# First cross attention in 64-row parts: scores, key norms and the last keys

## The chip, the cores and the metric

The kernel runs on one core of a Trainium2 chip. The metric is the device time of one execution in microseconds. Five engines work side by side and meet at semaphores: TensorE (PE; its weight loads are shown as PEld), VectorE (DVE), ScalarE (ACT), GpSimd (POOL) and SyncE (SP), which issues DMAs.

TensorE multiplies a stationary operand (lhsT, rows times columns) by a moving one (rhs, rows times N). [...] `128*64` in a profile line means 128 rows and 64 columns; "128x289" behind it is the moving operand, so N is 289. Everything is float32, and each float32 matmul of the program appears as two instructions.

## The reference

Six layers act on x (64 batches of 32 rows, width 256): cross attention, self attention, a mixture of 64 experts, a second cross attention, a latent self attention, a feed-forward layer. The change is within the first layer:

```python
xn = layernorm(x, ln_x_g, ln_x_b)          # context, 257 rows
ln = layernorm(latents, ln_l_g, ln_l_b)    # 32 rows
q = ln @ Wq                                # 16 heads of 64
kv = concat([xn @ Wkv, ln @ Wkv], axis=1)  # 289 keys
sim = einsum('bhid,bhjd->bhij', rmsnorm(q, qn_g) * 64 ** -0.5, rmsnorm(k, kn_g))
sim = where(padded_mask, sim, -max)
out = softmax(sim) @ v ;  return out @ Wout + bout
```

## The kernel before

**Stages.** `before` (the method, about the first 1,600 us) runs the first cross attention, the self attention and the routing; `experts` and `after` follow. In `before` there are 64 steps s, one for each batch; four batches make a tile t of 128 rows, with b = s mod 4. PE's instructions run in the order in which the program is written (a manual schedule). The other engines' order, and which engine an `nc.any` copy falls to (DVE or ACT), is set by a scheduler at build time.

**One step s** does, on PE: `keys(s+2)`, one slot, the transposes of `weigh(s)`, `norms(s+2)`, `values(s)`, `spread(s+2)`, a slot, `scores(s+2)`, `turn(s+3)`, and a third slot unless b is 3. A slot moves each pending generator one `yield` on: those of the queries of the next tile and of the output projection, self attention and routing of tiles that are done.

- `keys` (L160 psA<-xT,wk): 8 pairs of heads; for each, 2 accumulating matmuls give the pair's 128 key dimensions by 289 keys. ACT and DVE copy to kT in turn; after each fourth pair, ACT squares four pairs (L1164) into sq[0] and sq[1]. L1147 and L1148 fetch, by two DMAs on SP, the last 33 keys' rows (32 latents, one context row) into one of three buffers c3.
- `norms` (L1176): sums of squares over a head's 64 dimensions, by a 128 x 32 selector. 8 matmuls of form `128*32`: 4 column groups, 2 accumulating matmuls in each. Then a maximum on DVE (L1184) and a logarithm on ACT (L1185) give nk.
- `spread` (L1197, `32*128`): copies each norm to 32 rows; ACT takes exp(-0.5 .) into rk (L1198).
- `scores` (L1210): for each pair of heads one matmul of form `128*64`. Its stationary operand is qbd, in which the two heads' queries are block-diagonal, with zeros elsewhere. Two pairs fill the two column halves, so 8 matmuls fill 4 PSUM banks. DVE multiplies each bank by rk (L1217), POOL adds the mask (L1218), and `softmax_rows` follows.
- `weigh` (`keyed`, L195): 12 transposes give the weights with keys on partitions: 128, 128 and 33 keys (L196 copies them out; the last go to atl, whose other rows are zero).
- `values` (`weighed`): for each half kc of the 256 dimensions, 3 accumulating matmuls `128*128` with N = 512: two L160 psY<-at,cx and one L160 psY<-atl,c over the zero-padded c3. L205 copies the result to yT after each kc.
- `heads_out` reads yT by head (L160 psY<-yT,wv).
- `queries`, sixth slot: L1090 transposes q, and L1097 copies the parts of 64 rows into qbd.

PSUM has 8 banks, and `bank()` hands them out in a ring. qbd, c3 and atl are set to zero once by POOL (L373).

## Time and profile before

| What | Time or share |
|---|---|
| Median of 3 runs | 2926.83 us (2924.55 to 2929.37) |
| Profiled execution, its own time | 2931.93 us |
| Span of its instructions | 2930.2 us |
| PE busy | 2748.5 us, 94% |
| DVE, ACT, POOL busy | 56%, 42%, 29% |
| PE busy from 100 to 1580 us | 1434.47 of 1480 us, granted clock 1.00 |
| DVE, ACT, POOL busy, same stretch | 841.16, 743.97, 548.48 us |

A row of the timeline gives the start, how long the group lasts to the end of its last instruction, the engine, line, operation, result <- operands, shape and count. [...]

### The profile page before, as it was taken

How to read it: one execution, taken by the hardware profiler on the slowest of the kernel's cores; microseconds unless marked ns; L12 is line 12 of the kernel's file. 1: busy time of each engine (PE TensorE's matmuls, PEld its weight loads, DVE VectorE, ACT ScalarE, POOL GpSimd, SP SyncE). 2: the span in 40 equal slices, each digit the busy share in tenths (PEclk: the TensorE clock that was granted, in tenths of full speed). 3: DMA queues.
4: the chain of work that ended last, by engine and by line, in shares of the span. 5: the costliest groups of instructions: out<-in, count | busy, mean ns of one | idle time of the engine just before them, and what ended most of it. 6: DMA issues, size and time to landing. Idle time of an engine off the chain costs nothing. (4 is left out here: it accounts for less than half of the span.)

```text
span 2930.2 us, 56527 instructions
## 1 busy us (share of the span) xinstructions
PE 2748.5 (94%) x22362; PEld 1882.0 (64%) x22362; DVE 1649.3 (56%) x4401; ACT 1235.5 (42%) x3366; POOL 840.6 (29%) x819
## 2 busy tenths in 40 slices
PE   5999999999999999999999589999999999999995
PEld 3556666656666666666666368777677777777773
DVE  4445566556655655555555423356666666666664
ACT  3444554554455545445544223243333333333331
POOL 5322344234333423442342100222222122212010
PEclk8999999999999999999999789999999999999997
DMA  7000000000000000000000368521112212222110
GB/s 259 15 13 17 29 31 29 17 29 27 28 18 26 25 20 18 18 16 17 16 12 14 113 212 274 167 64 55 54 53 57 56 48 59 56 54 48 39 34 5
DMA packets 130956, 156.86 MB, mean 54 GB/s; under 512 B 20952, under 2 KB 113859, under 8 KB 130692
## 3 DMA queue, kind: packets, MB, share of 16 engines
q1 hardware_dynamic: 109188, 119.64, 13.1%
q0 software_dynamic: 12288, 25.21, 3.4%
q10 hardware_dynamic: 9216, 8.39, 0.8%
q8 instruction: 177, 2.90, 0.4%
q14 instruction: 87, 0.71, 0.1%
HBM read 121.63 MB, written 37.75 MB: 54 GB/s over the span
## 5 line engine op out<-in xcount | busy, mean ns | idle before, releaser
L160 PE MATMUL psA<-xT,wk 128*128 128x289 f32 x2048 | 516.6, 410 | 26.6 <-ACT xT L1136 16.5
L160 PEld LDWEIGHTS psA<-xT,wk 128*128 128x128 f32 x2048 | 386.7, 191 | 146.6 <-issue 37.0
L741 POOL DMA_INDIRECT y<-oute,idx x128 | 130.7, 1021 | 677.0 <-DVE x L752 475.3
L1218 POOL TENSOR_TENSOR rk<-rk,mb 128x1156 f32<-128x1156 f32 x64 | 158.0, 2469 | 433.7 <-DVE rk L1217 420.4
L160 PE MATMUL psY<-at,cx 128*128 128x512 f32 x512 | 248.1, 607 | 0.0
L160 PE MATMUL psA<-at,cx 128*128 128x512 f32 x512 | 236.2, 604 | 0.2 <-ACT at L1325 0.2
L160 PE MATMUL psY<-xT,qk 128*128 128x257 f32 x1024 | 234.4, 381 | 0.0
L160 PEld LDWEIGHTS psY<-xT,qk 128*128 128x128 f32 x1024 | 189.4, 190 | 28.6 <-issue 3.5
L205 ACT COPY yT<-psY 128x512 f32<-128x512 f32 x127 | 74.3, 585 | 241.0 <-PE psY L160 241.0
L1307 ACT ACTIVATE sim<-psY,mx 128x257 f32<-128x257 f32 x256 | 120.7, 473 | 129.5 <-DVE mx L1306 129.3
L176 ACT ACTIVATE rk<-rk,mx 128x289 f32<-128x289 f32 x256 | 134.0, 525 | 95.9 <-DVE mx L174 95.9
L160 PEld LDWEIGHTS psY<-at,cx 128*128 128x128 f32 x512 | 92.5, 190 | 121.5 <-issue 94.8
L1164 ACT ACTIVATE sq<-kT 128x1156 f32<-128x1156 f32 x128 | 148.9, 1164 | 18.6 <-DVE kT L1161 16.4
L160 PEld LDWEIGHTS psA<-at,cx 128*128 128x128 f32 x512 | 91.9, 189 | 97.4 <-issue 82.8
L606 POOL DMA_INDIRECT buf<-z,fi x128 | 126.4, 988 | 95.0 <-DVE fi L603 56.5
L1306 DVE TENSOR_REDUCE mx<-psY 128x1 f32<-128x257 f32 x256 | 102.5, 413 | 79.2 <-PE psY L160 79.2
L1337 DVE SCALAR_TENSOR_TENSOR yT<-at,xT,psA 128x512 f32<-128x512 f32 x128 | 94.3, 746 | 81.5 <-PE psA L160 80.0
L1210 PE MATMUL psB<-kT,qbd 128*64 128x289 f32 x1024 | 140.0, 415 | 0.0
L1159 ACT COPY kT<-psA 128x289 f32<-128x289 f32 x256 | 98.5, 388 | 95.8 <-PE psA L160 95.5
L160 PE MATMUL psY<-atl,c 128*128 128x512 f32 x256 | 130.7, 592 | 0.0
L160 PE MATMUL psY<-yT,wv 128*64 128x128 f32 x2048 | 120.5, 275 | 0.0
L1217 DVE TENSOR_TENSOR rk<-psB,rk 128x289 f32<-128x289 f32 x256 | 111.4, 451 | 15.2 <-ACT rk L1198 8.0
(256 smaller groups left out, 5181.3 us busy)
## 6 DMA issues: line engine op xcount, KB each, us to landing
cx<-in_ctx SPq DMA_DIRECT2D x128, 256.0 KB, 2.7
we<-in_m_ew SPq DMA_DIRECT2D x64, 384.0 KB, 5.0
xT<-in_ctxT SPq DMA_DIRECT2D x64, 257.0 KB, 3.1
buf<-zero SPq DMA_DIRECT2D x32, 256.0 KB, 3.9
be<-buf SPq DMA_DIRECT2D x64, 128.0 KB, 4.1
oute<-oe ACTq DMA_DIRECT2D x64, 128.0 KB, 4.8
mu<-in_mask SPq DMA_DIRECT2D x16, 128.5 KB, 3.0
x<-in_x SPq DMA_DIRECT2D x16, 128.0 KB, 3.7
```

The source lines that it names most:

```text
L160: self.nc.tensor.matmul(ps, lhsT=lhs[i], rhs=rhs[i], start=(i == 0), stop=(i == n - 1))
L176: nc.scalar.activation(sim[:, g, :], sim[:, g, :], AF.Exp, bias=mx[:, g : g + 1], accum_out=sm[:, g : g + 1])
L606: d = nc.gpsimd.indirect_dma_start(out=self.buf[:, :], out_offset=bass.IndirectOffsetOnAxis(ap=fi[:, k : k + 1], axis=0), in_=z[:, 0, :], ...
L741: nc.gpsimd.indirect_dma_start(out=y, out_offset=None, in_=self.oute[:, :], in_offset=bass.IndirectOffsetOnAxis(ap=self.idx[:, t, k : k + ...
L1159: nc.scalar.copy(kT[:, p, :], ps[:, :JK])
L1164: nc.scalar.activation(sq[p // 4], kT[:, p - 3 : p + 1, :], AF.Square)
L1210: nc.tensor.matmul(ps[odd * DH : (odd + 1) * DH, :JK], lhsT=qbd[:, 2 * g + odd, b, :, :].rearrange("p a b -> p (a b)"), rhs=kT[:, 2 * g + ...
L1217: nc.vector.tensor_tensor(sim[:, g, :], ps[:, :JK], sim[:, g, :], ALU.mult)
L1218: nc.gpsimd.tensor_tensor(sim, sim, mb[:, b, :].unsqueeze(1).to_broadcast([P, 4, JK]), ALU.add)
L1306: nc.vector.tensor_reduce(mx[:, g : g + 1], ps[:, :J], AX.X, ALU.max, negate=True)
L1307: nc.scalar.activation(sim[:, g, :], ps[:, :J], AF.Exp, bias=mx[:, g : g + 1], accum_out=sm[:, g : g + 1])
L1337: nc.vector.scalar_tensor_tensor(self.yT[:, c, :, b * S : (b + 1) * S], self.at[:, 2, :].rearrange("p (h i) -> p h i", h=H), xT[:, c, J - ...
```

## The change

Heads 2p and 2p+1 (even and odd) now lie apart, on row halves 0 to 63 and 64 to 127.

- `qbd` is replaced by qT, the transposed queries without the zeros, in a tile with two buffers; two copies of 128 partitions take the place of four of 64.
- `scores`: 16 matmuls of form `64*32` in place of 8 of `128*64`. In each half of the heads, 4 pairs p go to 4 column groups and even and odd go to the two row halves and to two banks.
- `norms`: even heads' sums go to PSUM rows 0 to 63, odd heads' to rows 64 to 127, as the new order of heads needs. 16 matmuls of form `64*32`, 4 accumulating in each of 4 parts (row half 0 with column groups 0 and 1, row half 64 with 2 and 3); two banks, two DVE maxima on 64 partitions each.
- The last 33 keys lie twice, on rows 0 to 32 and 64 to 96: `softmax_rows` writes their weights a second time with one more DVE operation, and the third group of transposes takes 128 columns in place of 33. c3 holds dimensions 0 to 127 on the first row half, 128 to 255 on the second (4 DMAs in place of 2).
- `weighed`: 2 matmuls `128*128` for each kc, then for kc = 0 and kc = 1 one matmul each of form `64*128` on the two row halves, then both copies to yT.
- rk becomes one of three fixed tiles of 4 x 384, set to zero once; at has 3 parts, atl is gone; `heads_out` follows the new order of heads in yT.

```diff
     def norms(self, s):
...
+        ps = [k.bank("psB") for _ in range(2)]
+        for p in range(4):
+            for half in range(2):
+                for odd in range(2):
+                    r, q = slice(DH * odd, DH * odd + DH), DH * odd + 32 * half
+                    nc.tensor.matmul(
+                        ps[odd][q : q + 32, :JK],
+                        lhsT=k.pair[p][r, :],
+                        rhs=sq[half][r, p, :],
+                        start=(p == 0),
+                        stop=(p == 3),
+                    )
+        nk = kp.tile([P, JK], F32, name="nk")
         for odd in range(2):
...
+            r = slice(DH * odd, DH * odd + DH)
+            nc.vector.tensor_scalar(nk[r, :], ps[odd][r, :JK], float(DH) * 1e-16, None, ALU.max)
         nc.scalar.activation(nk, nk, AF.Ln)
...
     def scores(self, s):
...
+        sim = whole[:, :, :JK]
+        for half in range(2):
+            ps = [k.bank("psB") for _ in range(2)]
+            for p in range(4):
+                for odd in range(2):
+                    r = slice(DH * odd, DH * odd + DH)
+                    nc.tensor.matmul(
+                        ps[odd][p * S : (p + 1) * S, :JK],
+                        lhsT=qT[r, 4 * half + p, b * S : (b + 1) * S],
+                        rhs=kT[r, 4 * half + p, :],
+                        start=True,
+                        stop=True,
+                    )
             for odd in range(2):
...
+                g = 2 * half + odd
+                nc.vector.tensor_tensor(sim[:, g, :], ps[odd][:, :JK], sim[:, g, :], ALU.mult)
         nc.gpsimd.tensor_tensor(sim, sim, mb[:, b, :].unsqueeze(1).to_broadcast([P, 4, JK]), ALU.add)
-        k.softmax_rows(sim, JK)
+        k.softmax_rows(sim, JK, whole[:, :, 2 * P + 64 : 2 * P + 64 + S + 1])
...
     def softmax_rows(self, sim, n, twice=None):
...
         nc.vector.reciprocal(sm, sm)
+        if twice is not None:
+            m = twice.shape[2]
+            nc.vector.tensor_tensor(
+                twice, sim[:, :, n - m :], sm.unsqueeze(2).to_broadcast([P, 4, m]), ALU.mult
+            )
...
     def weighed(self, yT, b, at, values, tail=None):
...
+        ps = [self.bank("psY") for _ in range(2)]
+        n = len(at)
         for kc in range(2):
...
+            for i in range(n):
+                nc.tensor.matmul(
+                    ps[kc],
+                    lhsT=values[i][:, kc * P : (kc + 1) * P],
+                    rhs=at[i],
+                    start=(i == 0),
+                    stop=(i == n - 1 and tail is None),
+                )
+        if tail is not None:
+            for kc in range(2):
+                r = slice(64 * kc, 64 * kc + 64)
+                nc.tensor.matmul(ps[kc], lhsT=tail[1][r, :], rhs=tail[0][r, :], start=False, stop=True)
+        for kc in range(2):
+            nc.any.tensor_copy(
+                yT[:, kc, :, b * S : (b + 1) * S], ps[kc].rearrange("p (h i) -> p h i", h=H)
+            )
...
     def keys(self, s):
...
-        nc.sync.dma_start(c3[:S, :], self.own[t][0][b * S : (b + 1) * S, 0, :])
-        nc.sync.dma_start(c3[S : S + 1, :], self.xl[s : s + 1, 0, :])
+        for c in range(2):
+            r, d = 64 * c, slice(c * P, (c + 1) * P)
+            nc.sync.dma_start(c3[r : r + S, :], self.own[t][0][b * S : (b + 1) * S, 0, d])
+            nc.sync.dma_start(c3[r + S : r + S + 1, :], self.xl[s : s + 1, 0, d])
```

More of the change, by code (lines that the diff above doesn't have):

```diff
@@ L43 @@
 C_PAIR = C_TRI + P
-C_SPREAD = C_PAIR + 2 * 32
+C_SPREAD = C_PAIR + 4 * 32
 C_B8 = C_SPREAD + P
@@ L61, in constants @@
     c[:, C_TRI:C_PAIR] = r[:, None] < r[None, :]
-    for a in range(2):
-        at = C_PAIR + a * 32
-        c[:, at : at + 32] = (2 * a + r[:, None] // DH) == np.arange(32)[None, :]
+    for a in range(4):
+        c[:, C_PAIR + a * 32 + a] = 1.0
     c[:, C_SPREAD:C_B8] = (r[:, None] % 32) == (r[None, :] // S)
@@ L166, in add_to_x, with softmax_rows @@
         nc.vector.tensor_tensor(xt, xt, ps, ALU.add)
-    def softmax_rows(self, sim, n):
+    def softmax_rows(self, sim, n, twice=None):
         nc = self.nc
@@ L179, in softmax_rows, with keyed @@
         nc.vector.reciprocal(sm, sm)
+        if twice is not None:
[3 more added lines that the diff above has]
+            )
         for g in range(4):
             nc.vector.tensor_scalar(sim[:, g, :], sim[:, g, :], sm[:, g : g + 1], None, ALU.mult)
-    def keyed(self, sim, sizes, tail=None):
+    def keyed(self, sim, sizes):
         nc = self.nc
-        at = self.atp.tile([P, len(sizes) - (tail is not None), 512], F32, name="at")
-        at = [at[:, j, :] for j in range(at.shape[1])]
-        if tail is not None:
-            at.append(tail)
+        at = self.atp.tile([P, len(sizes), 512], F32, name="at")
         k0 = 0
@@ L195, in keyed, with weighed, heads_out @@
                 nc.tensor.transpose(ps[:n, g * P : (g + 1) * P], sim[:, g, k0 : k0 + n], self.ident)
-            nc.any.tensor_copy(at[j][:n, :], ps[:n, :])
+            nc.any.tensor_copy(at[:n, j, :], ps[:n, :])
             k0 += n
-        return at if tail is not None else [at[j][:n, :] for j, n in enumerate(sizes)]
-    def weighed(self, yT, b, at, values):
-        for kc in range(2):
-            ps = self.bank("psY")
-            self.product(ps, [v[:, kc * P : (kc + 1) * P] for v in values], at)
-            self.nc.any.tensor_copy(
-                yT[:, kc, :, b * S : (b + 1) * S], ps.rearrange("p (h i) -> p h i", h=H)
+        return [at[:n, j, :] for j, n in enumerate(sizes)]
+    def weighed(self, yT, b, at, values, tail=None):
+        nc = self.nc
+        ps = [self.bank("psY") for _ in range(2)]
+        n = len(at)
+        for kc in range(2):
+            for i in range(n):
[13 more added lines that the diff above has]
+                yT[:, kc, :, b * S : (b + 1) * S], ps[kc].rearrange("p (h i) -> p h i", h=H)
             )
-    def heads_out(self, t, yT, wv, wo, bias):
+    def heads_out(self, t, yT, wv, wo, bias, split=False):
         nc = self.nc
@@ L217, in heads_out @@
                     h = 2 * (4 * half + p) + odd
+                    at = 8 * half + 4 * odd + p if split else h
                     self.product(
@@ L220, in heads_out @@
                         [wv[:, k, h * DH : (h + 1) * DH] for k in range(2)],
-                        [yT[:, k, h, :] for k in range(2)],
+                        [yT[:, k, at, :] for k in range(2)],
                     )
@@ L302, in run @@
         self.tri = c[:, C_TRI:C_PAIR]
-        self.pair = [c[:, C_PAIR + k * 32 : C_PAIR + (k + 1) * 32] for k in range(2)]
+        self.pair = [c[:, C_PAIR + k * 32 : C_PAIR + (k + 1) * 32] for k in range(4)]
         self.spread = c[:, C_SPREAD:C_B8]
@@ L366, in before @@
         nc.gpsimd.tensor_scalar(gam, gam, float(DH) ** 0.5, None, ALU.mult)
-        self.qbd = w.tile([P, 8, NB, 2, S], F32, name="qbd")
-        self.c3 = [w.tile([P, D], F32, name=f"c3{i}") for i in range(3)]
-        self.atl = [w.tile([P, 512], F32, name=f"atl{i}") for i in range(2)]
+        self.c3 = [w.tile([P, P], F32, name=f"c3{i}") for i in range(3)]
+        self.sim = [w.tile([P, 4, 3 * P], F32, name=f"sim{i}") for i in range(3)]
         zero = w.tile([P, D], F32, name="zero")
-        for x in (self.qbd, *self.c3, *self.atl, zero):
+        for x in (*self.c3, *self.sim, zero):
             nc.gpsimd.memset(x, 0.0)
@@ L481, in tail @@
     def tail(self, t, yT, wv, wo, bo, sw, swo, sg, gw):
-        yield from self.heads_out(t, yT, wv, wo, bo)
+        yield from self.heads_out(t, yT, wv, wo, bo, True)
         yield
@@ L1082, in queries @@
         yield
-        qbd = k.qbd
+        qT = k.wkx.tile([P, 8, P], F32, name="qTf")
         for half in range(2):
@@ L1094, in queries @@
                 )
-            for odd in range(2):
-                r = slice(DH * odd, DH * odd + DH)
-                nc.any.tensor_copy(
-                    qbd[r, 4 * half : 4 * half + 4, :, odd, :],
-                    ps[r, :].rearrange("p (m b i) -> p m b i", m=4, b=NB),
-                )
+            nc.any.tensor_copy(qT[:, 4 * half : 4 * half + 4, :].rearrange("p a b -> p (a b)"), ps)
         mu = k.wkx.tile([P, NB, J], U8, name="mu", bufs=1)
@@ L1108, in queries @@
         nc.gpsimd.tensor_scalar(mb[:, :, JK - 1 :], mu[:, :, J - 1 :], 1.0, BIG, ALU.subtract, ALU.mult)
-        self.own[t] = ln, lnT, qbd, mb
+        self.own[t] = ln, lnT, qT, mb
         yield
@@ L1171, in norms @@
         cx, c3, kT, sq = self.held[s]
-        ps = k.bank("psB")
-        for odd in range(2):
-            for g in range(4):
-                p = 2 * g + odd
-                nc.tensor.matmul(
-                    ps[g * 32 : (g + 1) * 32, :JK],
-                    lhsT=k.pair[odd],
-                    rhs=sq[p // 4][:, p % 4, :],
-                    start=(odd == 0),
-                    stop=(odd == 1),
-                )
-        nk = kp.tile([P, JK], F32, name="nk")
-        nc.vector.tensor_scalar(nk, ps[:, :JK], float(DH) * 1e-16, None, ALU.max)
+        ps = [k.bank("psB") for _ in range(2)]
[11 more added lines that the diff above has]
+        nk = kp.tile([P, JK], F32, name="nk")
+        for odd in range(2):
+            r = slice(DH * odd, DH * odd + DH)
+            nc.vector.tensor_scalar(nk[r, :], ps[odd][r, :JK], float(DH) * 1e-16, None, ALU.max)
         nc.scalar.activation(nk, nk, AF.Ln)
@@ L1192, in spread @@
         cx, c3, kT, nk = self.held[s]
-        rk = kp.tile([P, 4, JK], F32, name="rk", bufs=3)
-        for g in range(4):
-            r = slice(g * 32, (g + 1) * 32)
-            ps = k.bank("psR")
-            nc.tensor.matmul(ps[:, :JK], lhsT=k.spread[r, :], rhs=nk[r, :], start=True, stop=True)
-            nc.scalar.activation(rk[:, g, :], ps[:, :JK], AF.Exp, scale=-0.5)
+        rk = k.sim[s % 3]
+        for half in range(2):
+            for odd in range(2):
+                q = DH * odd + 32 * half
+                r = slice(q, q + 32)
+                ps = k.bank("psR")
+                nc.tensor.matmul(ps[:, :JK], lhsT=k.spread[r, :], rhs=nk[r, :], start=True, stop=True)
+                nc.scalar.activation(rk[:, 2 * half + odd, :JK], ps[:, :JK], AF.Exp, scale=-0.5)
         self.held[s] = cx, c3, kT, rk
@@ L1204, in scores @@
         t, b = divmod(s, NB)
-        _, _, qbd, mb = self.own[t]
-        _, _, kT, sim = self.held[s]
-        for g in range(4):
-            ps = k.bank("psB")
-            for odd in range(2):
-                nc.tensor.matmul(
-                    ps[odd * DH : (odd + 1) * DH, :JK],
-                    lhsT=qbd[:, 2 * g + odd, b, :, :].rearrange("p a b -> p (a b)"),
-                    rhs=kT[:, 2 * g + odd, :],
-                    start=True,
-                    stop=True,
-                )
-            nc.vector.tensor_tensor(sim[:, g, :], ps[:, :JK], sim[:, g, :], ALU.mult)
+        _, _, qT, mb = self.own[t]
+        _, _, kT, whole = self.held[s]
+        sim = whole[:, :, :JK]
+        for half in range(2):
+            ps = [k.bank("psB") for _ in range(2)]
+            for p in range(4):
+                for odd in range(2):
+                    r = slice(DH * odd, DH * odd + DH)
[6 more added lines that the diff above has]
+                    )
+            for odd in range(2):
+                g = 2 * half + odd
+                nc.vector.tensor_tensor(sim[:, g, :], ps[odd][:, :JK], sim[:, g, :], ALU.mult)
         nc.gpsimd.tensor_tensor(sim, sim, mb[:, b, :].unsqueeze(1).to_broadcast([P, 4, JK]), ALU.add)
-        k.softmax_rows(sim, JK)
+        k.softmax_rows(sim, JK, whole[:, :, 2 * P + 64 : 2 * P + 64 + S + 1])
     def weigh(self, s):
@@ L1224, in weigh @@
         cx, c3, _, sim = self.held.pop(s)
-        self.weights = k.keyed(sim, [P, P, S + 1], k.atl[s % 2]), [cx[:, 0, :], cx[:, 1, :], c3]
+        at = k.keyed(sim, [P, P, P])
+        self.weights = at[:2], [cx[:, 0, :], cx[:, 1, :]], (at[2], c3)
     def values(self, s):
```

## The prediction

> **What bounds the kernel now.** I read the page first, for which engine is busy and at what clock; then busy time by stretch, to see the stage that the change touches; then the groups of that stage by form, for PE's idle time; then the timeline of one step, for what each group costs.

> ```profile
> PE 2748.5 (94%) x22362; PEld 1882.0 (64%) x22362; DVE 1649.3 (56%) x4401; ACT 1235.5 (42%) x3366; POOL 840.6 (29%) x819
> ...
> PEclk8999999999999999999999789999999999999997
> ```
> ```profile
> 100.00:1580.00 1480.00, 1434.47 (x10494) 914.38 (x10493) 841.16 (x2421) 743.97 (x1972) 548.48 (x525) 1.00 0.07 21
> ```
> ```profile
> L160 PE MATMUL psA<-xT,wk 128*128 128x289 f32 x1909 | 478.8, 408 | 22.8 <-ACT xT L1136 12.7 <-issue 10.1
> ...
> L1176 PE MATMUL psB<-sq,c 128*32 128x289 f32 x960 | 82.8, 414 | 22.7 <-ACT sq L1164 22.7
> ```

> PE is busy 1434 of 1480 us here at full clock; DVE, next in the row, 57%. Of PE's 45.5 idle us, 22.8 stand before keys and 22.7 before norms. So a microsecond of PE work removed should be a microsecond of time, as long as the others' latencies stay covered. The step that starts at 725 us, PE alone:

> ```profile
> 725.26 1.47 PE L195 MATMUL psT<-c,rk 128*128 128x128 f32 x12
> 726.66 1.19 PE L1176 MATMUL psB<-sq,c 128*32 128x289 f32 x16
> 727.78 1.98 PE L160 MATMUL psY<-at,cx 128*128 128x512 f32 x4
> 729.60 1.02 PE L160 MATMUL psY<-atl,c 128*128 128x512 f32 x2
> 730.46 1.88 PE L160 MATMUL psY<-at,cx 128*128 128x512 f32 x4
> 732.17 1.02 PE L160 MATMUL psY<-atl,c 128*128 128x512 f32 x2
> 733.12 0.77 PE L1197 MATMUL psR<-nk,c 32*128 32x289 f32 x8
> 733.82 0.85 PE L534 MATMUL psB<-kbd,qT 32*32 32x64 f32 x64
> 734.61 2.17 PE L1210 MATMUL psB<-kT,qbd 128*64 128x289 f32 x16
> 736.71 0.66 PE L1133 MATMUL psT<-c,cx 128*128 128x128 f32 x4
> ```

> Start to next start: norms 727.78 - 726.66 = 1.12 us, values 733.12 - 727.78 = 5.34, scores 736.71 - 734.61 = 2.10. The price of one instruction that has the array to itself comes from the step before and from a row of the later stage:

> ```profile
> 716.94 8.04 PE L160 MATMUL psA<-xT,wk 128*128 128x289 f32 x32
> 724.82 0.60 PE L513 MATMUL psT<-c,qk 128*128 128x128 f32 x4
> ```
> ```profile
> 1980.12 1.47 PE L1324 MATMUL psT<-c,sim 128*128 128x128 f32 x12
> 1981.52 1.16 PE L1267 MATMUL psA<-qT,wkT 64*128 64x128 f32 x16
> 1982.61 3.70 PE L160 MATMUL psA<-at,cx 128*128 128x512 f32 x8
> ```

> With N = 289: 7.88 us / 32 = 0.246, which I call a slot. With N = 512: (732.17 - 730.46) / 4 = 0.428. So the 16 instructions of norms took 4 slots, 4 column groups at once (4 x 0.246 = 0.98, and 0.14 for the change of form); the 16 of scores took 8 slots (1.97), two column halves at once. L1267 shows two row halves at once: 16 instructions of N = 128 in 1.09 us, where one alone takes 0.109 (queries' transposes L1090, 8 in 0.87 us).

> **The change on PE, part by part.**

> Scores: 16 matmuls, 32 instructions, in two groups of 8 parts (4 column groups by 2 row halves) with 2 instructions each: 4 slots if all 8 stream together. From 2.10 to 2.10 - 4 x 0.246 = 1.12. Saved 0.98. No row shows form `64*32`. Bounds: at best these 4 slots; at worst no pairing of row halves, so 8 slots and nothing saved. Issue doesn't limit it: L534 passed 64 instructions in 0.79 us, 12 ns each, and 32 of those are 0.40 us. I take the 4 slots, since column groups (L1176), row halves (L1267) and both together (L534: 64 instructions in the time of about 15 alone, at 0.246 x 64/289 = 0.054 each) are all seen at once in rows.

> Norms: 32 instructions, but only 4 parts, each a chain of 4 matmuls with 2 instructions: 8 slots where there were 4. Halving the rows buys nothing, since each row half uses only two of the column groups. From 1.12 to 2.10; added 0.98. It cancels what scores save.

> Values: 12 instructions of N = 512 become 8 in the whole array and 4 in two row halves, which pair like L1267 in the same form: 10 slots. Saved 2 x 0.428 = 0.86. But there is one more change of form, into `64*128` before spread's `32*128`. Around L1267 it shows as extra time: L1324 1.40 - 12 x 0.109 = 0.09, L1267 1.09 - 8 x 0.109 = 0.22, the eight at,cx about 0.10; 0.41 for two changes, 0.20 each. (Bounds 0 to 0.20 here, as one end may be shared.) I take 0.20: values go from 5.34 to 4.68. Saved 0.66.

> Transposes: the third group takes 128 columns of weights; L195's instructions start 0.109 apart whether they have 33 or 128. Nothing.

> Sum: -0.98 + 0.98 - 0.66 = -0.66 us per step, times 64 steps = -42 us.

> [...]

> **The change beside PE.** DVE: the second maximum costs the whole 0.459 of L1184 again, since 64 partitions are not faster than 128 (qbd copy of 64x512: 0.683; at copy of 128x512: 0.683). The doubled weights, 128 x 132 elements, lie between 128x64 (L570, 0.25) and 128x256 (L166, 0.42): 0.3. Off DVE and ACT go 2 copies of some 0.6 us for each tile, 0.3 per step. Net about 0.45 us per step on engines 57% and 50% busy in a stage of 24.9 us per step: covered. Waits:

> - nk. Its logarithm ended at 728.85; spread starts at 733.12. That cover of 4.27 us shrinks by 0.66 and by 0.46. Only in the two steps of the start, where spread already waits 1.04 us, does the 0.46 show: +1 us.
> - Both yT copies now follow the last matmul. Both were on ACT, 0.58 each, the first behind kc = 1. ACT's next work, the four exponentials of spread (733.91 to 735.23), starts up to 0.58 later; behind them stand DVE's products L1217 and the copy of xT (737.40), for which PE waits in two steps of a tile (0.72 and 0.77 us). The transposes for xT would end near 736.4, the exponentials at 735.8. Covered, by half a microsecond. If the cover is gone in every step: +0.58 x 64 = 37 us.
> - Banks: norms take two, so the ring is one longer. Third and fourth banks of scores are those of values, free when the two copies end, about 0.75 and 1.35 us after the last values matmul; PE asks for them after spread (0.70) and half of scores (0.6). Just covered.
> - SP: two more DMAs of 0.51 to 0.58 us (L1147, L1148), past which only the load of cx is moved (L1114), which is five steps ahead. Nothing. POOL: 5,248 zeroed elements per partition for 4,096 (L373, 3.96 us), so 1.1 us more, while POOL then waits 7.84 us for gk. Nothing. At the start two of the four qbd copies that stand before the first xT copy (31.31 to 34.27) go: -1 us, which meets the +1 above.

> So the profiled execution goes from 2931.9 (span 2930.2 and 1.7 around it) to 2890. It stood 5.1 us above the median, so the forecast is 2926.8 - 42 = 2885.

> **Rivals.**

> 1. Slower: in form `64*32` the two row halves of a column group take turns. Place: scores, 8 slots as before, 2.10 us. Then +0.98 - 0.66 = +0.32 per step, +20 us: 2947. It decides from 7 slots on (-0.25 + 0.98 - 0.66 = +0.07). Against it: L1267 and L534; for it: no row has this form, and eight streams of 289 columns at once are nowhere seen.
> 2. Given back: the late yT copies push the exponentials, products and banks, and PE waits for them. Half of the 0.58 per step gives 2885 + 19 = 2904; all of it 2922, no change. For it: cover of half a microsecond. Against: most steps have a slot's PE work there.
> 3. More gained: the change of form costs nothing in values (-0.86, -55 us) and the waits before keys shrink by a few: 2868.

> **How the numbers follow.** Forecast, 2868 to 2896 with rival 3 as its low end: 0.68. Partly given back, to 2915: 0.10. Wholly given back, around 2922 to 2932: 0.08. Rival 1, around 2947: 0.14. What a measurement of this kernel can tell from no change is about 0.2%, 6 us, so faster is below 2921: 0.78; same 0.08; slower 0.14. Range 2868 to 2915, which leaves out the last two cases.

> **What would show it.** Right: norms with 32 instructions at 2.1 us to the next start, scores with 32 at 1.1, values at 4.7 with a row of 4 instructions `64*128`; PE busy about 2707; idle before keys and norms near 45 us still. Wrong: scores near 2.1 (rival 1); idle time in front of psA, psB or psR rows above 1 us in many steps, ended by ACT or DVE (rival 2); norms well under 2.1, which would mean that parts stream in a way that I haven't read from the rows.

## The result and the profile after

The changed kernel takes 2979.86 us (median; 2977.31 to 2981.95), the kernel before 2927.84 us beside it on the same chip: a ratio of 1.018 (95% interval 1.016 to 1.020), so 52 us **slower**. The forecast was 2885 us, 42 us faster, and the range ended at 2915. The profiled execution took 2978.31 us (span 2976.5).

First the page's engine row, and the row of busy time by stretch (columns as in the prediction: PE, PEld, DVE, ACT, POOL, granted clock), both after:

```profile
PE 2735.5 (92%) x24410; PEld 1857.8 (62%) x24410; DVE 1732.1 (58%) x4526; ACT 1204.7 (40%) x3337; POOL 840.4 (28%) x819
```
```profile
100.00:1580.00 1480.00, 1386.30 (x11869) 867.18 (x11869) 898.34 (x2481) 689.78 (x1881) 543.55 (x522) 0.99 0.07 21
```

Over the whole execution PE is busy 13 us less (2748.5 before), where 42 were forecast (2707), and it waits more: in the same 1480 us idle goes from 45.5 to 93.7 us. The granted clock, 1.00 before, reads 0.99. The groups by form in the same stretch, after:

```profile
L159 PE MATMUL psA<-xT,wk 128*128 128x289 f32 x1856 | 473.9, 414 | 43.1 <-issue 25.4 <-ACT xT L1149 17.7
...
L1193 PE MATMUL psB<-sq,c 64*32 64x289 f32 x1856 | 154.5, 414 | 48.1 <-ACT sq L1179 48.1
...
L1235 PE MATMUL psB<-kT,qTf 64*32 64x289 f32 x1824 | 68.8, 410 | 0.0
L220 PE MATMUL psY<-at,c 64*128 64x512 f32 x230 | 65.1, 641 | 0.0
```

The two waits that stood there before, 22.8 us before keys and 22.7 before norms, are now 43.1 and 48.1. ACT ends the second; for the first, see below.

A **tile** is 4 steps. I cut the PE rows into groups, from the start of each to the start of the next (a row's length runs into the next row: before, norms start at 726.66 and last 1.19 us, and values start at 727.78), take idle time out, and average the 12 tiles that follow 300 us. In us for one tile:

| PE | Before | After | Difference | Forecast |
|---|---|---|---|---|
| scores | 8.40 | 4.55 | -3.85 | -3.92 |
| values (at,cx and last keys) | 21.39 | 18.76 | -2.63 | -2.64 |
| norms, without their wait | 5.16 | 10.03 | +4.88 | +3.92 |
| keys, without their wait | 31.54 | 32.25 | +0.70 | 0 |
| idle before keys (xT) | 1.49 | 3.05 | +1.56 | 0 |
| idle before and within norms (sq) | 1.33 | 2.82 | +1.49 | 0 |
| self attention's scores (kbd), their wait, transposes | | | +0.54 | 0 |
| period | 99.71 | 102.40 | +2.69 | -2.64 |

Sixteen tiles make 43 of the 46 us by which the two profiled executions differ. So the prices of scores and values held to a few hundredths. Norms cost 0.96 us per tile more than forecast, and the waits more than doubled.

**Why the squares come late.** Follow one step, here with keys at 743.89 us (before: 716.94, the step that the prediction shows). PE, then DVE, POOL and ACT of the kernel after; each row has start, length, engine, line, operation, and in brackets the wait and what ended it:

```profile
741.39 1.20 PE L1235 MATMUL psB<-kT,qTf 64*32 64x289 f32 x32
742.53 0.66 PE L1146 MATMUL psT<-c,cx 128*128 128x128 f32 x4
...
743.89 8.04 PE L159 MATMUL psA<-xT,wk 128*128 128x289 f32 x32
...
753.61 0.68 PE L1193 MATMUL psB<-sq,c 64*32 64x289 f32 x4
755.07 2.14 PE L1193 MATMUL psB<-sq,c 64*32 64x289 f32 x28 [0.78 <-ACT sq L1179]
757.14 3.70 PE L210 MATMUL psY<-at,cx 128*128 128x512 f32 x8
760.77 1.13 PE L220 MATMUL psY<-at,c 64*128 64x512 f32 x4
761.83 0.77 PE L1219 MATMUL psR<-nk,c 32*128 32x289 f32 x8
```
```profile
743.34 1.54 DVE L1244 TENSOR_TENSOR sim<-psB,sim 128x289 f32<-128x289 f32 x4
...
747.63 1.36 DVE L174 TENSOR_REDUCE mx<-sim 128x4 f32<-128x1156 f32 x1 [2.15 <-POOL sim L1245]
...
751.45 0.30 DVE L182 TENSOR_TENSOR sim<-sim,sm 128x132 f32<-128x132 f32 x1
751.78 1.25 DVE L186 TENSOR_SCALAR sim<-sim,sm 128x289 f32<-128x289 f32 x4
752.95 0.81 DVE L1176 COPY kT<-psA 128x289 f32<-128x289 f32 x2
```
```profile
744.96 2.63 POOL L1245 TENSOR_TENSOR sim<-sim,mb 128x1156 f32<-128x1156 f32 x1 [0.43 <-DVE sim L1244]
```
```profile
746.12 0.40 ACT L1174 COPY kT<-psA 128x289 f32<-128x289 f32 x1 [1.82 <-PE psA L159]
749.02 0.54 ACT L176 ACTIVATE sim<-sim,mx 128x289 f32<-128x289 f32 x1 [2.50 <-DVE mx L174]
...
751.11 0.38 ACT L1174 COPY kT<-psA 128x289 f32<-128x289 f32 x1
751.52 1.17 ACT L1179 ACTIVATE sq<-kT 128x1156 f32<-128x1156 f32 x1
...
753.85 1.17 ACT L1179 ACTIVATE sq<-kT 128x1156 f32<-128x1156 f32 x1 [0.57 <-DVE kT L1176]
```

The same ACT rows before:

```profile
719.17 0.40 ACT L1159 COPY kT<-psA 128x289 f32<-128x289 f32 x1 [0.83 <-PE psA L160]
720.53 0.54 ACT L176 ACTIVATE rk<-rk,mx 128x289 f32<-128x289 f32 x1 [0.97 <-DVE mx L174]
...
725.02 0.40 ACT L1159 COPY kT<-psA 128x289 f32<-128x289 f32 x1 [0.53 <-PE psA L160]
725.45 1.17 ACT L1164 ACTIVATE sq<-kT 128x1156 f32<-128x1156 f32 x1
```

ACT keeps the order that the build gave it, and the four exponentials of the softmax stand between the first copy of the new keys and the others. They need the whole chain behind the scores: DVE's four products, POOL's mask (2.4 to 2.6 us), DVE's maximum (1.36). The chain from the end of the last product to the end of the second square took 10.03 us before and 10.14 after. But the 10.03 hold 0.53 us in which ACT's last copy waits for PE's keys (row 725.02): there the keys themselves set the square, and the chain behind the scores had 0.53 us to spare. Before, the square ended at 726.62, and PE's norms began at 726.66 (the prediction's first timeline): a **cover of 0.04 us**. After, the scores take PE 0.98 us less, and the products, which used to run beneath them, end 1.34 us later against the start of keys. The last copies now come from DVE at 752.95, behind the softmax's own products (L182, the doubled weights, and L186). The square ends at 755.02, 1.41 us after PE has come to the norms. Of the 1.45 us of cover lost, 0.81 are the products' 1.34 less the 0.53 to spare, and 0.64 are a longer chain (10.14 for 9.50 of work). The cover in the four steps of a tile (PE free for norms, less the end of the second square; medians of the 12 tiles):

| Step of the tile | Before | After |
|---|---|---|
| queries' transposes before keys | 0.04 | -1.41 |
| self attention's scores before keys | 0.97 | -0.46 |
| self attention's output before keys | 2.61 | 0.18 |
| routing between keys and norms | -1.96 | -2.65 |

Only the last of these showed as a wait before. The second row is 0.97 after, as before, in the five tiles whose keys ran at half the clock (below).

In the two middle steps the chain itself is longer, 10.61 us for 9.59 and 12.51 for 11.52. In each, a DVE operation now meets POOL's mask and ends only behind it, in all 12 tiles (by 0.5 us and by 0.02). In the step with self attention's scores, DVE and POOL after, then DVE before, where the mask was over at 740.77:

```profile
768.25 3.14 DVE L283 TENSOR_TENSOR e<-e,smh 128x512 f32<-128x512 f32 x1
```
```profile
768.20 2.64 POOL L1245 TENSOR_TENSOR sim<-sim,mb 128x1156 f32<-128x1156 f32 x1 [15.69 <-DVE smh L260]
```
```profile
742.08 0.68 DVE L264 TENSOR_TENSOR e<-e,smh 128x512 f32<-128x512 f32 x1
```

DVE's maximum then starts 0.84 us behind the mask, where it was 0.04. In the next step L110 takes 1.96 us beside the mask, 0.16 without it. With e's softmax later (an experiment below) L283 takes 0.68 us again, and that step's chain 9.82. No run changed this meeting alone.

**Why xT comes late.** In the step with self attention's scores, ACT's order differs. After:

```profile
766.34 0.63 ACT L258 ACTIVATE e<-e 128x512 f32<-128x512 f32 x1 [1.78 <-DVE e L257]
766.87 0.57 ACT L1149 COPY xT<-psT 128x512 f32<-128x512 f32 x1
...
767.54 2.68 PE L159 MATMUL psA<-xT,wk 128*128 128x289 f32 x10 [1.95 <-issue]
```

and before:

```profile
737.40 0.59 ACT L1136 COPY xT<-psT 128x512 f32<-128x512 f32 x1 [1.84 <-PE psT L1133]
737.88 0.64 ACT L239 ACTIVATE e<-e 128x512 f32<-128x512 f32 x1
...
738.09 1.22 PE L160 MATMUL psA<-xT,wk 128*128 128x289 f32 x4 [0.72 <-issue]
```

The scheduler has put the exponential of e, which waits 1.78 us for DVE, ahead of the copy that PE needs. PE's wait goes from 0.72 to 1.95 us. ("issue" is what the view names where no releaser is found; the copy's end is the event that fits.) In the step with self attention's output it goes from 0.77 to 1.10: L111 and L112 of the next layer norm, which need a chain on DVE that starts with PE's output product, stand ahead of the copy in both kernels. Before, ACT was through with them 0.48 us ahead of the transposes; after, the scores between the two are shorter, and the copy waits for them.

**And PE at half its clock.** Three neighbouring stretches of the kernel after, in the view of busy time by stretch:

```profile
866.07:869.48 3.41, 1.46 (x36) 0.67 (x21) 3.18 (x8) 1.54 (x5) 0.00 (x0) 1.00 0.04 10
869.48:872.90 3.42, 3.42 (x7) 2.50 (x8) 3.39 (x4) 0.00 (x0) 2.63 (x1) 0.50 0.01 2
872.90:876.31 3.41, 3.41 (x15) 2.66 (x14) 3.02 (x5) 1.72 (x6) 0.00 (x0) 1.00 0.00 0
```

In the first PE waits 1.95 us for xT and is busy 1.46 of 3.41 us. In the second it is busy throughout, but the granted clock is 0.50, and keys' instructions start 0.481 us apart in place of 0.243. In the clock records of the two traces such stretches are 3.41 us long or a multiple (6.83, 10.24, 13.65). From 100 us to the last keys the kernel before has none, the kernel after seven places (23.9 us in all, so at most 11.9 us lost). That is the +0.70 of keys, in 5 of 12 tiles. A tile with such a stretch takes 103.02 us, one without 101.95: 1.07 us more and not the 1.71 of half a stretch, since PE then comes to the norms behind the squares and they stream in one piece (2.09 us for 2.75).

### The profile page after: what moved, and what is told of

Its sections match the earlier page's. It is cut to its first block, busy times and chain, and to the rows that moved or that the text cites. A ratio compares the mean times of both kernels' runs of the same rounds, so it can differ in the third digit from the quotient of the medians.

```text
span 2976.5 us, 60850 instructions
## 1 busy us (share of the span) xinstructions
PE 2735.5 (92%) x24410; PEld 1857.8 (62%) x24410; DVE 1732.1 (58%) x4526; ACT 1204.7 (40%) x3337; POOL 840.4 (28%) x819
## 5 line engine op out<-in xcount | busy, mean ns | idle before, releaser
L159 PE MATMUL psA<-xT,wk 128*128 128x289 f32 x2048 | 523.9, 414 | 48.7 <-issue 27.3
L1245 POOL TENSOR_TENSOR sim<-sim,mb 128x1156 f32<-128x1156 f32 x64 | 155.9, 2436 | 466.1 <-DVE smh L260 219.7
L210 PE MATMUL psY<-at,cx 128*128 128x512 f32 x512 | 236.7, 605 | 0.0
L1193 PE MATMUL psB<-sq,c 64*32 64x289 f32 x2048 | 172.2, 417 | 54.3 <-ACT sq L1179 54.1
L176 ACT ACTIVATE sim<-sim,mx 128x289 f32<-128x289 f32 x256 | 134.1, 526 | 110.4 <-DVE mx L174 110.4
L111 ACT ACTIVATE rs<-rs 128x1 f32<-128x1 f32 (+2 forms) x177 | 35.6, 202 | 296.9 <-DVE rs L110 296.9
L1193 PEld LDWEIGHTS psB<-sq,c 64*32 64x32 f32 x2048 | 65.2, 108 | 138.9 <-ACT sq L1179 77.0
L1203 DVE TENSOR_SCALAR nk<-psB 64x289 f32<-64x289 f32 x128 | 58.6, 458 | 107.8 <-PE psB L1193 105.8
```

What stands on the lines that cost most here:

```text
L159: self.nc.tensor.matmul(ps, lhsT=lhs[i], rhs=rhs[i], start=(i == 0), stop=(i == n - 1))
L176: nc.scalar.activation(sim[:, g, :], sim[:, g, :], AF.Exp, bias=mx[:, g : g + 1], accum_out=sm[:, g : g + 1])
L210: nc.tensor.matmul(ps[kc], lhsT=values[i][:, kc * P : (kc + 1) * P], rhs=at[i], start=(i == 0), stop=(i == n - 1 and tail is None),)
L1193: nc.tensor.matmul(ps[odd][q : q + 32, :JK], lhsT=k.pair[p][r, :], rhs=sq[half][r, p, :], start=(p == 0), stop=(p == 3),)
L1245: nc.gpsimd.tensor_tensor(sim, sim, mb[:, b, :].unsqueeze(1).to_broadcast([P, 4, JK]), ALU.add)
```

## The experiments

Each was compared with the kernel before on its own chip. Beside four of the runs (norms twice, half of the scores, norms behind values, turn first on the last keys alone) that kernel took 2948.9 us, beside the others 2926 to 2929, so go by ratios and differences; "low" is the time between 100 us and the last keys in which the profiled execution had half the clock (half of it, at most, is lost). The clock's part was seen only behind the last of them, so the expectations know nothing of it.

| Run | Time, us | Ratio (95% interval) | Against before, us | Low, us |
|---|---|---|---|---|
| last keys alone | 2904.21 | 0.9918 (0.9898 to 0.9939) | -25 | 6.8 |
| norms twice, on before | 3017.41 | 1.0231 (1.0210 to 1.0253) | +68 | 3.4 |
| half of the scores, on before | 2906.83 | 0.9857 (0.9833 to 0.9881) | -42 | 6.8 |
| scores and norms, no last keys | 3007.82 | 1.0266 (1.0248 to 1.0284) | +80 | 37.5 |
| last keys, norms twice | 2958.73 | 1.0110 (1.0086 to 1.0133) | +31 | 6.8 |
| last keys, half of the scores | 2865.71 | 0.9785 (0.9768 to 0.9801) | -62 | 3.4 |
| after | 2979.86 | 1.0179 (1.0161 to 1.0196) | +52 | 23.9 |
| after, scores issued twice | 3081.42 | 1.0523 (1.0495 to 1.0550) | +152 | 23.9 |
| after, turn first | 2954.01 | 1.0084 (1.0064 to 1.0105) | +25 | 30.7 |
| after, DVE lightened | 2982.66 | 1.0184 (1.0162 to 1.0206) | +53 | 58.0 |
| after, norms behind values | 2997.15 | 1.0168 (1.0148 to 1.0187) | +48 | 23.9 |
| after, e's softmax later | 2965.69 | 1.0128 (1.0111 to 1.0145) | +37 | 37.5 |
| the same, copies of keys first | 2973.52 | 1.0155 (1.0134 to 1.0176) | +45 | 51.2 |
| after, norms in 8 parts | 2943.20 | 1.0049 (1.0032 to 1.0066) | +15 | 34.1 |
| after, old norms | 2955.87 | 1.0090 (1.0074 to 1.0107) | +30 | 71.7 |
| the same, e's softmax later | 2928.11 | 1.0005 (0.9995 to 1.0014) | +2 | 34.1 |

**The parts alone.** Last keys alone: scores, norms, spread and queries from the kernel before; `heads_out` unsplit, qbd back.

```diff
-            self.product(ps, [v[:, kc * P : (kc + 1) * P] for v in values], at)
...
+                nc.tensor.matmul(ps[kc], lhsT=tail[1][r, :], rhs=tail[0][r, :], start=False, stop=True)
```

> The last keys on both row halves alone; scores, norms and qbd as in the kernel before. Theory A (place): each matmul costs what was forecast, but the time that scores give lies in front of PE's waits for xT and for the squares and is lost there, while the time that norms take lies behind the wait for the squares and is paid in full; values stands in front of no wait, so its 0.66 us per step are all gained: 2928 - 42 = 2886. Theory B (DVE's load): the second maximum (0.46) and the doubled weights (0.30) make DVE late with the copies for which PE waits; here only 0.30 of 0.76 stays, so some 40% of the loss of 94 us against the forecast: about 2920. Theory C (order on ACT): both yT copies late and the build's order of ACT, with the xT copy behind an exponential that waits for DVE; the late yT copies are here too: 2900 to 2930.

-25 us. Per tile PE gained what was priced: last keys -3.00, at,cx +0.37, self attention's scores +0.28, and the waits stayed or shrank (1.49 for xT, 0.73 for squares) but for 0.19 before self attention's scores. The rest of the forecast's 42 went at the start, where keys begin 4.4 us later, and to 6.8 us of half clock before 220 us.

Norms' matmuls twice, in the kernel before:

```diff
-        for odd in range(2):
+        for i in range(4):
+            odd = i % 2
             for g in range(4):
```

> The kernel before, with norms' 8 matmuls issued twice over the same result: 8 slots in place of 4, as in the changed kernel, and nothing else. If the added time is paid in full because it lies behind the wait for the squares: 2929 + 63 = 2992, up to 3005 with more pieces cut by that wait. If another engine sets the pace further on, part of it is absorbed: 2950 to 2975.

+68 us: the price in full (63) and a little more. The four slots lie behind the wait for the squares, where nothing absorbs them.

Half of the scores:

```diff
-            ps = k.bank("psB")
+            ps = k.bank("psB") if g < 2 else held[g - 2]
+            held.append(ps)
...
+                if g > 1:
+                    break
```

> The kernel before with half of the scores left out: groups 2 and 3 take the results of groups 0 and 1, so scores take 4 slots in place of 8, and DVE, ACT and POOL do what they did. If PE's time is what counts: 2929 - 63 = 2866. If the chains on ACT and DVE that end in the copy of xT and in the squares keep their own time, the saving is lost in two or three of four steps: 2895 to 2920.

-42 of 63 us. PE's wait for xT stayed (1.45 us per tile): in this build ACT copies xT ahead of the exponential of e. So shorter scores do not lengthen that wait by themselves; the order on ACT does (1.23 of the 1.56 us, by the run with e's softmax later). The cover of the squares fell to -0.10, 0.23, 2.37 and -1.31 us, and new waits of 1.64 us per tile stood within values.

**Undone or pushed, on the changed kernel.** Scores issued twice, which gives PE's slots back to their old place:

```diff
-            for p in range(4):
+            for p in (0, 1, 2, 3, 0, 1, 2, 3):
```

> The changed kernel, with every matmul of scores issued twice over the same result, so that scores take 8 slots again (+0.98 us of PE per step, +63 us if all of it shows). Theory A: the waits that scores opened close again (3.3 us of idle time per tile and 0.7 us of restart, 16 tiles: 64 us), so most of the 63 is absorbed: 2980 to 3000. Theory B: DVE sets the pace at the waits, so PE work in front of them is absorbed as well: about 2985. Theory C: the order on ACT stays what it is, the xT copy waits for the same DVE work, which waits for PE's scores in turn: most is added, 3020 to 3043.

+100 us on the change, not absorbed. That lost time can be refilled in its place does not hold as a sum: the wait for xT grew to 3.50 us per tile, and new ones came within keys (1.60) and the transposes (1.32). For the squares alone it holds: in the step with the queries' transposes the last product ends 0.98 us earlier against the start of keys (0.01 for 0.99), the chain is as long as in the change (10.11 us), and the cover comes back from -1.41 to -0.41. The squares' wait falls from 2.82 to 1.44 us per tile, about that of before (1.33). Turn ahead of scores:

```diff
+            if s + 3 < n:
+                cross.turn(s + 3)
             slot()
             if s + 2 < n:
                 cross.scores(s + 2)
```

> The changed kernel, with the transposes for the next keys (turn) in front of scores instead of behind them, so that scores cover the copy of xT. Theory A: the idle 3.05 us per tile before keys and 0.70 us of restart go, 16 tiles: -60, if the wait for the squares doesn't grow: 2920; if that wait takes what is freed, 2950. Theory B: the copies for xT are on ACT, DVE stays as late as it was with the squares' inputs, so the time goes into that wait: 2960 to 2980. Theory C: the copy comes before the exponential that held it: 2930.

-27 us on the change. The wait for xT went wholly (3.05 us per tile), and keys are back at 31.54 us, but a part came back elsewhere: norms +0.96 us per tile, transposes +0.49 and 0.35 of wait; the squares' wait stayed (3.04). The same on last keys alone gained nothing:

> The last keys on both row halves alone, with turn in front of scores. The 1.49 us per tile before keys go: 2904 - 24 = 2880. If the time is taken by the wait for the squares, 2890 to 2904.

2925.41 us, ratio 0.9925 (0.9906 to 0.9944), -23. There the wait for xT was small, and new waits took its place (1.73 us per tile for squares, where it is 0.73 with last keys alone, and 0.71 for copies of at).

DVE's load off: the logarithm reads PSUM on ACT with a tiny bias in place of two maxima, and POOL copies the doubled weights.

```diff
-            nc.vector.tensor_scalar(nk[r, :], ps[odd][r, :JK], float(DH) * 1e-16, None, ALU.max)
-        nc.scalar.activation(nk, nk, AF.Ln)
+            nc.scalar.activation(nk[r, :], ps[odd][r, :JK], AF.Ln, bias=k.tiny[r, :])
```

> The changed kernel with DVE's added work taken off: the logarithm reads the norms from PSUM with a tiny added constant instead of the maximum on DVE (0.92 us per step less on DVE, 0.45 more on ACT), and POOL copies the doubled weights. Theory A: the place of PE's work is unchanged, so 2965 to 2980. Theory B: the cause is gone and the forecast comes back in large part: 2890 to 2925. Theory C: 2970 to 2985, ACT has a little more.

No gain in time; by that alone DVE's load would not matter. The clock says otherwise. Two stretches, one tile apart, each with the one behind it:

```profile
867.56:870.97 3.41, 1.46 (x14) 1.09 (x9) 3.35 (x9) 1.10 (x2) 0.17 (x1) 1.00 0.00 0
870.97:874.39 3.42, 3.42 (x9) 2.40 (x8) 3.42 (x3) 0.40 (x1) 2.46 (x1) 0.50 0.00 0
969.96:973.37 3.41, 1.45 (x14) 1.08 (x9) 3.36 (x9) 1.10 (x2) 0.16 (x1) 1.00 0.00 0
973.37:976.79 3.42, 3.42 (x9) 2.40 (x8) 3.42 (x3) 0.40 (x1) 2.47 (x1) 0.50 0.02 5
```

PE's idle time fell by 0.86 us per tile, but keys took 0.98 us more, since every tile from 359 us on has half the clock behind its wait for xT. These stretches follow each other at 102.4 us, 30 times 3.413, and the tile's period is 102.48: the one tile behind 200 us without a half-clock stretch takes 101.00 us, and all that follow lie near that multiple. By PE's idle time DVE's load was worth some 14 us (16 x 0.86), and keys at half clock took them (16 x 0.98).

Norms behind values, so that the squares have time:

```diff
             cross.values(s)
+            if s + 2 < n:
+                cross.norms(s + 2)
+            if s + 3 < n:
+                cross.turn(s + 3)
             if s + 2 < n:
                 cross.spread(s + 2)
```

> The changed kernel with norms behind values and turn in front of spread and scores, so that PE has work while xT and the squares are made; between norms and spread stand a slot and turn. If the waits before keys and norms and the pieces that they cut are the whole loss (7.7 us per tile), 2979 - 124 = 2855 and the forecast comes back; a new wait of spread for nk, up to 1.5 us in the steps where the slot holds no PE work, would leave 2880 to 2920. If DVE's or ACT's throughput is the bound, it stays above 2950.

The waits for squares and xT went, and norms fell to 8.35 us per tile. But PE now waits 4.00 us per tile in values, for the most part for the copies of at, 2.45 in the transposes of the weights and 1.13 within keys; 7.85 us idle in all. As these rows read, the norms' place had been cover for them.

ACT's order: self attention's softmax is written one slot later, and PE's order stays.

```diff
-        recip = self.softmax_heads(e)
         yield
+        recip = self.softmax_heads(e)
         yield from self.attend_self(t, e, recip, swo, None)
```

> The changed kernel, with the softmax of the self attention one slot later in the program, so that on ACT the copy of xT comes before the exponential of e that held it; PE's instructions are the same in the same order. Against the kernel before, beside which it runs (the changed kernel stood at +52). Theory C (order on ACT makes the longer wait for xT): the wait of 1.95 us in this step goes back to 0.72 and about 0.4 us of restart go, 16 tiles: -25, so +27. Theory D (scores are shorter, the chains on DVE and ACT take their own time, so the wait stays or moves): +45 to +52.

-15 us on the change. The wait for xT goes back from 3.05 to 1.82 us per tile and keys to 31.54 us. But the half clock now falls behind the wait for squares, in more tiles: 37.5 us low for 23.9. So the order is worth more with the clock left out: tiles without a half-clock stretch take 100.45 us for 101.95, 24 us in 16 tiles. That holds all that follows from the order, the meeting of L283 with the mask too.

Then copies of keys and squares with a higher priority at build time, on that kernel, on before (2924.04 us, 0.9991 (0.9982 to 1.0001)) and on last keys alone (2906.86, 0.9926 (0.9909 to 0.9943)):

> As the last, and the copies to kT and the squares come first among what is ready on DVE and ACT. Theory C: the longer wait for the squares (1.5 us per tile and 1.1 us of pieces) goes too, 16 tiles: another -35 or so, and the changed kernel comes to 0 to -10 against the kernel before. Theory D: the work that they overtake (exponentials, at copies, maxima) is needed by PE a little later and the time shows there: +25 to +45.

> Control: the kernel before with the same order of precedence for the copies to kT and the squares. Its wait before norms is 1.36 us per tile: at most -22; if the wait isn't one of order, 0 or a loss as what is overtaken comes late.

> The last keys on both row halves alone, with the same precedence. The last keys alone stood at -25 and wait 0.84 us per tile for the squares: -25 to -38; if what is overtaken comes late, -10 to -25.

No gain in any; in the changed kernel the low time rose to 51.2 us, again at 102.4 us distances; its tiles without half clock take 100.62 us for 100.45, so the clock hides no gain there. Why priority gains nothing was not followed further.

**Pairs of parts.** Single parts, two of them stand-ins, sum to +1 us; the whole is +52. Which two hurt each other? Scores and norms, with the last keys as before:

> The changed kernel without its last-keys part: scores and norms in 64-row by 32-column parts, the last keys as in the kernel before (tail over 128 zero-padded rows, weights written once, yT copied after each half). Alone against the kernel before, the single parts gave: last keys -25 us, norms (by doubled matmuls) +68, scores (by half of them left out) -42; their sum is +1, while the whole change is +52. So 51 us are an effect of parts on each other. Theory 1, scores and norms are the pair that hurts (the time that the scores free comes back as waits before the next keys and the norms): +26 by the sum plus most of 51, so about 1.02 to 1.026 of the kernel before (+60 to +77). Theory 2, the last keys are the partner (their late yT copies and third DVE product push the chain behind them): about +26 or 1.009, and then the last keys cost 26 on top of it in the change.

Last keys with doubled norms, and last keys with half of the scores:

> Last keys in the new way on the kernel before, and each matmul of its norms issued twice (8 slots in place of 4, so a stand-in for the new norms; each pair of heads' sums come twice as large). Sum of the two single parts: -25 + 68 = +43, 1.015. If last keys and norms hurt each other (theory 2): up to +90, 1.03. If they merely share waits, 1.012 to 1.015.

> Last keys in the new way on the kernel before, and half of its scores left out (groups 2 and 3 take the results of groups 0 and 1), as a stand-in for scores in 4 slots. Sum of the two single parts: -25 - 42 = -67, 0.977. By PE's prices alone (-42 and -63): -105, 0.964. If PE's savings share the same slack of the other engines, so that the second is worth less than the first: -42 to -55, 0.981 to 0.986; then a part of the missing 51 us is this slack used twice.

+80, +31 and -62, by sums of single parts +26, +43 and -67. So the 51 us are not between the last keys and the others: the last keys take off 28 us from the pair, about as much as alone (25), and scores with norms are 54 us over their sum. Whether norms are the partner is seen below. The pair has the covers of the change (-1.04, -0.32, 0.29, -2.43 us), its wait for xT (3.05 us per tile) and 37.5 us of half clock. A stretch of it, norms behind the squares:

```profile
734.00:737.60 3.60, 2.07 (x18) 1.12 (x19) 3.57 (x13) 3.30 (x8) 2.69 (x4) 1.00 0.27 94
737.60:741.00 3.40, 3.40 (x28) 1.24 (x23) 0.68 (x3) 0.38 (x1) 3.08 (x3) 0.52 0.27 94
```

The doubled norms and halved scores are no more than stand-ins: with half of the scores left out, the last product ends 0.42 us after the start of keys and not 0.99, and ACT's order is the old one.

**Norms made short again.** In 8 parts (4 slots), spread over 64 rows (4 slots for 2):

```diff
+        for j in range(2):
+            for c in range(4):
...
-                        ps[odd][q : q + 32, :JK],
+                        ps[odd][32 * c : 32 * c + 32, :JK],
```

> The changed kernel with norms in 8 parts of 64 rows by 32 columns (4 slots, as scores) in place of 4 parts (8 slots); each bank then holds 128 rows, and spread takes 64 rows for 32 (4 slots for 2). By price, per step: norms -0.98, spread +0.49, in all -31 us from the changed kernel: 2949, 1.007. Theory: norms behind the wait for the squares are paid in full and more where they come in pieces, so -31 to -50 (0.999 to 1.007). Rival: another wait takes it up, and it stays within 10 us of the changed kernel (1.014 to 1.018), which would say that the stage is set by the other engines' chains and not by PE's work.

-37 us on the change, as priced (-31) and 6 more. The covers are the same to 0.03 us, the waits too (6.00 us per tile for 6.07). So norms' slots are paid in full, and the waits do not come from them: with norms as short as before they are all there. Then the old norms with a spread in the new order of heads, and with e's softmax later as well:

```diff
-                nc.tensor.matmul(ps[:, :JK], lhsT=k.spread[r, :], rhs=nk[r, :], start=True, stop=True)
+                nc.tensor.matmul(ps[:, :JK], lhsT=k.spread[odd][r, :], rhs=nk[r, :], start=True, stop=True)
```

> The changed kernel with the norms of the kernel before: 8 matmuls of 128 rows by 32 columns in one bank (4 slots), one maximum, and spread over 64 rows with two selectors, which puts the heads into the new order (4 slots for 2). By price from the changed kernel: norms -0.98, spread +0.49 per step, so -31 us, as with the norms in 8 parts, which measured -37; here DVE has a maximum of 0.46 us and ACT half a logarithm less per step. If these chains set when the squares come, a further -10 to -20: 2922 to 2933, 0.998 to 1.002. If only PE's slots count: 2943, 1.005, as there.

> As the run with the old norms in the changed kernel, and the self attention's softmax one slot later, so that on ACT the copy of xT stands ahead of the exponential of e (which took the changed kernel from +52 to +37). If the two gains add: another -14 to -20 us, 2905 to 2929, 0.992 to 1.000; with the price of PE alone the best that a kernel with the new scores and last keys could do here is 2838 + 24 for spread, 0.978. If the wait comes back elsewhere, 0 to -5.

The first was 12 us slower than norms in 8 parts by the ratios (15 by the medians), although DVE has less to do: the same waits, but 71.7 us at half clock for 34.1, in 19 places, so up to 19 us more lost. The second gained 28 us on the first, more than e's softmax later had given alone, and the half clock falls by 37.6 us, up to 19 of time; tiles without it take 97.78 us for 99.27, the same 1.5 us as above. It is no faster than the kernel before.

These runs also answer the question of pairs. Single parts for the scores (-42), the last keys (-25) and spread at its measured cost (+1.49 us per tile with norms in 8 parts, +1.89 with the old norms: 24 and 30 us) sum to -43 and -37. Measured are +15 and +30, so 58 and 67 us over, with norms as short as before (17 and 36 of it at most are the clock's). The excess does not need the longer norms. It comes with the new scores in every run that has them, and halved scores, whose products end earlier and whose order on ACT is the old one, do not have it. New scores alone were not run. **The fastest of the kernels that leave nothing out is the last keys alone, ratio 0.992; with turn first or the copies first it can't be told from that.**

## Why the prediction was wrong

- **Scores, -0.98 us per step:** right on PE (-0.96). The 8 parts stream together: 32 instructions take 1.14 us, which is 4 slots (0.98) and 0.16 more; rival 1, row halves in turn, is out.
- **Norms, +0.98:** right where nothing waits (2.09 us for 1.11). Where the second square is late, four instructions run ahead of the wait and cover no slot: 2.75 us. That happened in one step of a tile before and in two or three after, hence +1.22.
- **Values, -0.66:** right (-0.66), and as a part alone 25 of its 42 us came through.
- **"Idle before keys and norms near 45 us still":** this step failed. It became 91 us in the same stretch. The sentence it rests on is the first one, "a microsecond of PE work removed should be a microsecond of time, as long as the others' latencies stay covered". I listed covers of nk, yT, banks and SP, all of work that the change adds or moves. I did not list the cover of work that stays, against PE work that goes: the second square, 0.04 us ahead of PE in one step, with 0.53 to spare in the chain behind the scores, and 0.97 in the next. These rows were there to be read, beside those I quoted. DVE's 0.45 us per step, "covered" by my count, was not: with DVE lightened, PE's idle time is 0.86 us per tile less.
- **Late yT copies (rival 2):** they happen, ended by ACT before self attention's scores, and cost 0.19 us of wait and 0.28 of cost per tile, some 7 us in all. The loss is at the place that rival 2 names as last, PE waiting for ACT, but not by its cause.
- **ACT's order:** I took it as fixed. The build puts the exponential of e ahead of the xT copy, and this is worth 15 to 28 us by the two runs that undo it, 24 in both by tiles without half clock.
- **The clock:** 1.00 in the row that I read, and no term for it. At most 12 us here (the five stretches behind 300 us cost 1.07 each), and up to 36 in an experiment.

By size, per tile: 5.33 us lie between forecast and result (+2.69 for -2.64). Waits are 3.24 of them (1.56 xT, 1.49 squares, 0.19 yT), norms behind their wait 0.96, half clock 0.70, self attention's scores 0.28, and 0.15 is left for others. Shown by runs are the order on ACT and norms' price. That shorter scores take the squares' cover is shown for the step with the queries' transposes: the run with scores issued twice gives 1.00 us of cover back for 0.98 us of scores. In the other steps it is read from the timelines, where the chain is longer too, by 1.02 and 0.99 us in the two middle ones, with a DVE operation in each that takes 3.14 us for 0.68 and 1.96 for 0.16 beside POOL's mask; what each part weighs there stays open. What stays open is how much of the 24 us of this wait (16 x 1.49) a schedule could regain: each order that I tried moved the wait to another place. A longer lead, squares of a later step, was not tried.

## What to carry to other kernels

Before pricing a microsecond that is taken from the bounding engine, measure the cover of every operand that it takes from others within that loop, also where no wait is shown, and the time to spare in the chain that makes it: here 0.04 and 0.53 us stood in front of a saving of 0.98. Here time added behind a wait was paid in full and time removed in front of it was not, so two changes that cancelled in busy time did not cancel. A stand-in that only leaves work out does not move the other engines as the real change does. And after an edit read the other engines' order again, and the clock, before an experiment that "gains nothing" is held against a theory.
